# Last-layer layernorm variance from chunk sums in a bidirectional minGRU kernel: Squares on ScalarE and accumulating DMAs for four turned token tiles

## The chip, the cores and the metric

One core of a Trainium2 chip runs the whole kernel. The time is the device time of one execution in microseconds (us). TensorE is called PE in the profile (its weight loads PEld), VectorE DVE, ScalarE ACT, GpSimd POOL and SyncE SP. All data are float32. "A measurement" of the kernel before is a median of 3 executions: 1724.67 us, from 1724.2 to 1725.33.

## What is computed

Eight items of 512 tokens with 512 features (B = 8, S = H = 512) go through a block of two residual branches. The part that the change touches is the first branch, a stack of four bidirectional minGRU layers, fused by one matrix. Cut to what matters:

```python
def _mingru(x, Wz, bz, Wh, bh):
    z = sigmoid(einsum('bsi,hi->bsh', x, Wz) + bz)
    h_tilde = tanh(einsum('bsi,hi->bsh', x, Wh) + bh)
    a = clip(1.0 - z, CLAMP_LO, CLAMP_HI)
    return _linear_scan(a, z * h_tilde)          # h_t = a_t * h_(t-1) + z_t * h~_t

def _stack(x, ...):
    h = x
    for i in range(4):
        h_new = _mingru(h, Wz[i], bz[i], Wh[i], bh[i])
        if i > 0:
            h_new = h_new + h
        h = _layernorm(h_new, gamma, beta)
    return h

h_comb = concatenate([_stack(x), flip(_stack(flip(x)))], axis=-1)
x = x + einsum('bsi,hi->bsh', h_comb, fusion_W) + fusion_b      # x is normalised ahead of the stack
x = x + ffn(_layernorm(x))                                      # ternary weights, GELU, layernorm
```

The same matrix serves as Wz and Wh here, and both directions share their weights. The layernorm after the last layer needs, for each token, the mean and the variance over 512 features. The kernel folds the mean into the fusion weights, so that only 1/sqrt(variance + 1e-5) of each token is left to find; fusion multiplies its result with it.

## The kernel before

A stream is one item in one direction, `(b, d)`; there are 16. Its state `h` is kept transposed: features on the partitions, in four chunks of 128, and the 512 tokens along the free axis, since the scan runs over tokens. The layernorm between layers wants the features along the free axis. So each of the four tiles of 128 tokens is "turned" (four PE transposes into one PSUM bank `pt`, `turned`, L294), DVE takes its statistics (`stats`, L153: BN_STATS, aggregate, and the addition of eps; POOL raises to the power -0.5), ACT writes the normalised token tile, and four more transposes turn it "back" (ACT evicts the bank `pf` with gamma and beta, L316).

The order of the work is written out by hand as a series of steps: `slot` (L407) is one step, and `now[0]` counts them. The instructions are put on each engine's queue in exactly this order. In one step: the gate chunk of one stream (`gates`, L422: eight PE matmul instructions into `u`; ACT computes `a`, `t` and `z` from it, `factors`, L441), then what is due of the two queues `turns` and `backs` (`shares`, at most `cap` of each, as soon as their step has come), then on DVE the product `z*t` and the scan of the chunk (`product`, `scan`), then what was put off as "resid", then the closing work on ACT of the turns and backs (the eviction of `pf`, the normalised token tile). ACT may run ahead of DVE by as many chunks as there are buffers of `a` (3) and `t` (2); PE may run ahead of ACT by four buffers of `u`.

Items go in pairs. Within a pair the streams come in the order (b, 0), (b, 1), (b+1, 0), (b+1, 1), four gate chunks each, so a layer of a pair takes 16 steps. In the last layer (L520) the residual sum of a stream can't be added chunk by chunk, because `h` is still read by the gates of the later chunks; so the sums `h[c] += z[c]` come one a step from the step of the stream's last gate chunk on, in "resid". They are done in place, and `h` is the input of fusion. `norm_last` (L339) then queues four turns, from the fifth step after the last gate chunk on, one a step: transposes, statistics, and the power into column `t` of `rsv`. No token tile is written. In the same steps the turns of items to come (`norm_x`, statistics of `x` for the first layer, tile `x`) and, in the first pair, small pieces that prepare the ternary weights (`pieces`; ACT: absolute values of `pwa`) are mixed in.

`fusion` (L533) follows, four steps an item (16 PE matmul instructions each, `pu`), and in the pairs before the last the steps of the next pair's first layer are put between them. `need` (L273) at the start of an item's fusion makes steps of turns alone until no turn of its two streams is left. DVE then adds `pu * rsv` to the row of `x`, and SP stores it. After the last pair the FFN runs to the end of the kernel; it is not touched.

The buffers that the change touches: `tok` (10 tiles of 128 x 512, counted in `held`), `z` (16 tiles, counted in `zlive`), `ps_t` (2 PSUM banks). No DMA is issued by POOL.

Of the kernel before, what the change touches and what calls it, by code (L numbers as in the profile page):

```python
# [9 lines left out]
F32 = mybir.dt.float32  # L10
F32R = mybir.dt.float32r
AF = mybir.ActivationFunctionType
ALU = mybir.AluOpType
AX = mybir.AxisListType
PSUM = bass.MemoryType.PSUM

P = 128
LN_EPS = 1e-5
# [6 lines left out]
def kernel(  # L25
# [26 lines left out]
    nc = tc.nc  # L52
    B, S, H = x.shape
    L = gru_wT.shape[0]
    F = fc_wT.shape[1]
    NC_ = H // P
    NT = S // P
# [7 lines left out]
    small = ctx.enter_context(tc.tile_pool(name="small", bufs=8))  # L65
# [4 lines left out]
    tokp = ctx.enter_context(tc.tile_pool(name="tok", bufs=TOK))  # L70
# [48 lines left out]
    for i in range(2):  # L119
        s = const.tile([P, P], F32, name=f"fpick{i}")  # L120
# [24 lines left out]
    ident = const.tile([P, P], F32, name="ident")  # L145
# [3 lines left out]
    mhalf = const.tile([P, 1], F32, name="mhalf")  # L149
# [3 lines left out]
    def stats(src, name, rs=None, shift=True):  # L153

        st = small.tile([P, 6], F32, tag="st", name=f"st_{name}")
        nc.vector.bn_stats(st, src)  # L156
        mv = small.tile([P, 2], F32, tag="mv", name=f"mv_{name}")
        nc.vector.bn_aggr(mv, st)  # L158
        if rs is None:
            rs = small.tile([P, 1], F32, tag="rs", name=f"rs_{name}")  # L160
        ve = small.tile([P, 1], F32, tag="ve", name=f"ve_{name}")
        nc.vector.tensor_scalar(ve, mv[:, 1:2], LN_EPS, None, ALU.add)
        nc.gpsimd.tensor_tensor(rs, ve, mhalf, ALU.pow)  # L163
        if not shift:
            return rs, None
        nmu = small.tile([P, 1], F32, tag="nmu", name=f"nmu_{name}")
        nc.vector.tensor_scalar(nmu, mv[:, 0:1], -1.0, None, ALU.mult)  # L167
        return rs, nmu

    def normalise(dst, src, rs_nmu, name):  # L170
        rs, nmu = rs_nmu
        nmr = small.tile([P, 1], F32, tag="nmr", name=f"nmr_{name}")
        nc.scalar.activation(nmr, nmu, AF.Copy, scale=rs)
        nc.scalar.activation(dst, src, AF.Identity, bias=nmr, scale=rs)  # L174
# [39 lines left out]
    with rec:  # L214
        gp = rec.enter_context(tc.tile_pool(name="gate", bufs=3))
        ps_u = rec.enter_context(tc.tile_pool(name="ps_u", bufs=4, space=PSUM))
        ps_t = rec.enter_context(tc.tile_pool(name="ps_t", bufs=2, space=PSUM))
# [4 lines left out]
        now = [0]  # L222
        state = {}
        rsv = {}
        turns, backs = [], []

        held = [0]
# [32 lines left out]
        zlive = [0]  # L260

        left = {}

        def queue(q, key, at, piece, go):
            left[key] = left.get(key, 0) + 1
            q.append((at, piece, key, go))
# [6 lines left out]
        def need(*keys):  # L273

            while any(left.get(k) for k in keys):
                slot(None, 2)

        def tokens(source, tok, rs, name):

            def go():  # L280
                src = source()
                found = stats(src, name, rs, tok is not None)
                if tok is None:
                    return lambda: None
                held[0] += 1

                def last():
                    tile_ = tokp.tile([P, H], F32, tag="tok", name=f"tok_{name}")
                    normalise(tile_, src, found, name)
                    tok.append(tile_)  # L290
                return last
            return go

        def turned(zs, t, name, frees=0):  # L294
            def source():
                if t == NT - 1:
                    zlive[0] -= frees
                spare = name.startswith("00_0") and t > 1
                pt = (ps_f if spare else ps_t).tile([P, H], F32, tag="pf" if spare else "pt", name=f"pt_{name}")
                for c in range(NC_):  # L300
                    nc.tensor.transpose(pt[:, ts(c, P)], zs[c][:, ts(t, P)], ident)  # L301
                return pt
            return source
# [21 lines left out]
        def norm(s, zs, tag, pause, pair=1):  # L325

            toks, at = Tokens(), now[0] + pause

            def dst():
                if s not in state:  # L330
                    state[s] = hp.tile([P, NC_, S], F32, tag="h", name=f"h_{s[0]}{s[1]}")
                return state[s]

            for t in range(NT):
                queue(turns, s, at, t // pair, tokens(turned(zs, t, f"{tag}_{t}", NC_), toks, None, f"{tag}_{t}"))
            for c in range(NC_):
                queue(backs, s, toks, c // pair, back(toks, dst, c, True, f"{tag}_{c}"))

        def norm_last(s, tag):  # L339
            rsv[s] = small.tile([P, NT], F32, tag="rsv", name=f"rsv_{tag}")  # L340
            zs = [state[s][:, c, :] for c in range(NC_)]
            for t in range(NT):
                queue(turns, s, now[0] + NC_ + 1, t, tokens(turned(zs, t, f"{tag}_{t}"), None, rsv[s][:, t : t + 1], f"{tag}_{t}"))

        rx, scale = {}, {}

# [44 lines left out]
        stages = []  # L391
# [15 lines left out]
        def slot(work=None, cap=1, long=False):  # L407

            end = work() if work is not None else None
            due("factors")  # L410
            if long:
                due("scans")
            last = shares(cap) + x_shares()
            due("scans")
            if end is not None:
                end()
            due("resid")
            for f in last:
                f()
            now[0] += 1  # L420
# [82 lines left out]
        def layer(s, l):  # L503
            while s not in state:
                slot(None, 2)
            need(s)
            zs = []
            h = state[s]
            for o in range(NC_):
                def scans(a, z, o=o):  # L510
                    scan(z, a, z, s[1] == 1)
                    zs.append(z)
                    if l < L - 1:
                        nc.vector.tensor_tensor(z, z, h[:, o, :], ALU.add)  # L514
                    elif o == NC_ - 1:

                        for c in range(NC_):
                            def sums(c=c):
                                zlive[0] -= 1
                                nc.vector.tensor_tensor(h[:, c, :], zs[c], h[:, c, :], ALU.add)  # L520
                            stages.append((now[0] + c, "resid", sums))
                slot(gates(h, l, o, f"{s[0]}{s[1]}_{l}_{o}", scans))

                if s[0] < 2 and (l == L - 1 or o % 2) and len(extra) > 2 * NW or s == (B - 2, 1) and l == L - 1:
                    pieces(1)
            now[0] -= 1
            if l < L - 1:
                norm(s, zs, f"{s[0]}{s[1]}_{l}", 2)
            else:
                norm_last(s, f"{s[0]}{s[1]}_{l}")  # L530
            now[0] += 1

        def fusion(b):  # L533
            hs, rs = [], []

            def tile_of(t):
                def work():
                    if t == 0:
                        need((b, 0), (b, 1))
                        hs.extend(state.pop((b, d)) for d in range(2))  # L540
                        rs.extend(rsv.pop((b, d)) for d in range(2))
                    row = xs["f", b, t]
                    nc.vector.tensor_tensor(row, row, fb, ALU.add)
                    pieces((1, 2, 1, 0, 2, 2, 2, 2)[t + (b % 2) * NT])
                    pus = []
                    for d in range(2):
                        pu = ps_u.tile([P, H], F32, tag="u", name=f"pu_{b}_{t}_{d}")
                        for c in range(NC_):
                            nc.tensor.matmul(  # L549
                                pu, lhsT=hs[d][:, c, ts(t, P)], rhs=fw[:, d * NC_ + c, :],  # L550
                                start=(c == 0), stop=(c == NC_ - 1),
                            )
                        pus.append(pu)

                    def end():
                        for d in range(2):
                            nc.vector.scalar_tensor_tensor(
                                row, pus[d], rs[d][:, t : t + 1], row, ALU.mult, ALU.add
                            )
                        nc.sync.dma_start(out=x1[b][t], in_=row)  # L560
                    return end
                return work
            return [tile_of(t) for t in range(NT)]


        sums = {n: const.tile([P, NW], F32, name=f"sums_{n}") for n in ("fc", "pw")}
# [187 lines left out]
    for i in range(2):  # L754
        s = const.tile([P, P], F32, name=f"pick{i}")
# [132 lines left out]
    for j in range(ends):  # L888
        b, k = divmod(j, NF)
# [81 lines left out]
```

## Time and profile before

| | |
|---|---|
| median of 3 executions | 1724.67 us |
| the profiled execution | 1725.0 us, of which 1723.0 us from the first to the last instruction |
| granted PE clock | 1.000 |
| GRU part, fusion included | up to about 1228 us |
| FFN part | from about 1228 us to the end |

The last layer from its first residual sum to the start of fusion, one stretch for each pair:

| pair, stretch (us) | PE busy | DVE busy | ACT busy | POOL busy |
|---|---|---|---|---|
| first, 224 to 277 | 53.00 | 47.73 | 35.06 | 8.09 |
| second, 524 to 576 | 51.72 | 46.87 | 26.29 | 8.01 |
| third, 823 to 875 | 52.00 | 46.88 | 26.96 | 7.99 |
| fourth, 1121 to 1173 | 51.39 | 49.21 | 31.14 | 6.52 |

Busy time counts overlapping instructions once. [...]

How to read the lines: a group row of the page gives line, engine, operation, output <- input, shapes and count, then busy time, the mean of one in ns, the idle time just before it and what ended that. A timeline row gives start, duration, engine, line, operation, and in brackets the idle time before it with its releaser. A row of the chain gives start, duration, engine and line of one piece of the chain of work that ended last.

### The profile page before, as it was taken

How to read it: one execution, taken by the hardware profiler on the slowest of the kernel's cores; microseconds unless marked ns; L12 is line 12 of the kernel's file. 1: busy time of each engine (PE TensorE's matmuls, PEld its weight loads, DVE VectorE, ACT ScalarE, POOL GpSimd, SP SyncE). 2: the span in 40 equal slices, each digit the busy share in tenths (PEclk: the TensorE clock that was granted, in tenths of full speed). 3: DMA queues.
4: the chain of work that ended last, by engine and by line, in shares of the span. 5: the costliest groups of instructions: out<-in, count | busy, mean ns of one | idle time of the engine just before them, and what ended most of it. 6: DMA issues, size and time to landing. Idle time of an engine off the chain costs nothing.

```text
span 1723.0 us, 19728 instructions
## 1 busy us (share of the span) xinstructions
PE 1704.6 (99%) x6424; PEld 1039.2 (60%) x6424; DVE 1452.1 (84%) x2865; ACT 1067.0 (62%) x1836; POOL 214.6 (12%) x334
## 2 busy tenths in 40 slices
PE   8999999999999999999999999999999999999998
PEld 4455554455555445555544555554688888888887
DVE  7989989889998998999899899996468778768876
ACT  3898883468886245888624688861266566566654
POOL 2111111111111111111111111111000000000000
PEclk9999999999999999999999999999999999999999
DMA  7002221250000125000012201102201101101100
GB/s 269 19 25 80 98 86 43 68 189 1 1 13 19 55 68 189 1 1 17 14 55 80 92 10 40 74 1 97 75 1 50 49 1 49 50 12 39 49 19 31
DMA packets 46454, 91.73 MB, mean 53 GB/s; under 512 B 5264, under 2 KB 5264, under 8 KB 45328
## 3 DMA queue, kind: packets, MB, share of 16 engines
q1 hardware_dynamic: 45488, 88.91, 15.3%
q10 hardware_dynamic: 864, 1.57, 0.3%
q8 instruction: 50, 0.82, 0.2%
q14 instruction: 52, 0.43, 0.1%
HBM read 65.30 MB, written 25.17 MB: 53 GB/s over the span
## 4 chain that ended last, share of the span: by engine, by line
PE 75%; DVE 19%; issue 4%; ACT 1%; POOL 0%; DMA 0%; DVEq 0%; POOLq 0%
PE u L427 29%; PE ph L788 12%; PE po L815 12%; PE pu L549 9%; PE pt L301 5%; DVE z L455 4%; PE pf L310 4%; PE u L470 3%; DVE st L156 3%; DVE z L451 2%; DVE zf L455 1%; DVE a L450 1%; DVE mv L158 1%; PE py L199 1%; DVE z L514 1%
## 5 line engine op out<-in xcount | busy, mean ns | idle before, releaser
L427 PE MATMUL u<-h,gw 128*128 128x512 f32 x768 | 345.5, 592 | 0.0
L427 PE MATMUL u<-xT,gw 128*128 128x512 f32 x768 | 345.4, 592 | 0.0
L455 DVE TENSOR_TENSOR_SCAN z<-a,z 128x512 f32<-128x512 f32 x224 | 274.1, 1224 | 7.6
L792 ACT ACTIVATE g<-ph 128x512 f32<-128x512 f32 x128 | 76.4, 597 | 242.1 <-PE ph L788 242.1
L427 PEld LDWEIGHTS u<-h,gw 128*128 128x128 f32 x768 | 138.7, 190 | 139.2 <-issue 138.7
L427 PEld LDWEIGHTS u<-xT,gw 128*128 128x128 f32 x768 | 138.7, 190 | 139.2 <-issue 138.0
L444 ACT ACTIVATE a<-u,ngb 128x512 f32<-128x512 f32 x192 | 131.5, 685 | 143.0 <-PE u L427 142.5
L163 POOL TENSOR_TENSOR rs<-ve,mhalf 128x1 f32<-128x1 f32 x192 | 123.0, 641 | 713.4 <-DVE nmu L167 656.9
L156 DVE BATCH_NORM_STATS2 st<-pt 128x6 f32<-128x512 f32 x256 | 177.1, 692 | 40.3 <-PE pt L301 39.8
L815 PE MATMUL po<-pwq,ghi 128*128 128x512 f32 x512 | 203.5, 397 | 0.0
L788 PE MATMUL ph<-yhi,fcq 128*128 128x512 f32 x512 | 199.7, 390 | 0.0
L815 PE MATMUL po<-pwq,glo 128*128 128x512 f32 x512 | 199.6, 390 | 0.0
L788 PE MATMUL ph<-ylo,fcq 128*128 128x512 f32 x512 | 199.4, 389 | 0.0
L451 DVE TENSOR_TENSOR z<-z,t 128x512 f32<-128x512 f32 x224 | 153.4, 685 | 8.5 <-ACT z L446 8.3
L174 ACT ACTIVATE tok<-pt,nmr,rs 128x512 f32<-128x512 f32 x192 | 149.2, 777 | 6.4
L803 DVE TENSOR_TENSOR acc<-acc,g 128x512 f32<-128x512 f32 x112 | 77.3, 690 | 87.9 <-ACT g L792 86.9
L446 ACT ACTIVATE z<-u,gb 128x512 f32<-128x512 f32 x192 | 132.2, 689 | 0.0
L445 ACT ACTIVATE t<-u,gb 128x512 f32<-128x512 f32 x192 | 130.7, 681 | 0.0
L301 PEld LDWEIGHTS pt<-ident,z 128*128 128x128 f32 x640 | 78.4, 141 | 82.4 <-issue 47.5
L549 PE MATMUL pu<-fw,xT 128*128 128x512 f32 x256 | 115.2, 593 | 0.0
L549 PE MATMUL pu<-fw,h 128*128 128x512 f32 x256 | 115.1, 592 | 0.0
L470 PE MATMUL u<-xT,gw 128*128 128x512 f32 x256 | 114.6, 593 | 0.3 <-DVE gw L672 0.3
(138 smaller groups left out, 2550.7 us busy)
## 6 DMA issues: line engine op xcount, KB each, us to landing
xn<-in_x_dram SPq DMA_DIRECT2D x32, 256.0 KB, 4.6
xf<-in_x_dram SPq DMA_DIRECT2D x32, 256.0 KB, 6.2
x<-xf SPq DMA_DIRECT2D x32, 256.0 KB, 2.0
xy<-x SPq DMA_DIRECT2D x32, 256.0 KB, 4.3
out_dram<-xy SPq DMA_DIRECT2D x32, 256.0 KB, 2.0
xT<-in_xt_dram SPq DMA_DIRECT2D x7, 1024.0 KB, 7.7
fca<-in_fc_wT_dram SPq DMA_DIRECT2D x16, 256.0 KB, 2.9
pwa<-in_proj_wT_dram SPq DMA_DIRECT2D x16, 256.0 KB, 2.6
```

Of the source, the lines that this page charges most:

```text
L156: nc.vector.bn_stats(st, src)
L174: nc.scalar.activation(dst, src, AF.Identity, bias=nmr, scale=rs)
L301: nc.tensor.transpose(pt[:, ts(c, P)], zs[c][:, ts(t, P)], ident)
L427: nc.tensor.matmul(u, lhsT=gw[l][:, c, ts(o, P)], rhs=h[:, c, :], start=(c == 0), stop=(c == NC_ - 1),)
L444: nc.scalar.activation(a, u, AF.Sigmoid, bias=ngb[:, l, o : o + 1], scale=-1.0)
L446: nc.scalar.activation(z, u, AF.Sigmoid, bias=gb[:, l, o : o + 1])
L451: nc.vector.tensor_tensor(z, z, t, ALU.mult)
L455: nc.vector.tensor_tensor_scan(dst[:, d], a[:, d], z[:, d], 0.0, ALU.mult, ALU.add)
L470: nc.tensor.matmul(u, lhsT=gw[0][:, c, ts(o, P)], rhs=xT[b][:, c, :], start=(c == 0), stop=(c == NC_ - 1),)
L549: nc.tensor.matmul(pu, lhsT=hs[d][:, c, ts(t, P)], rhs=fw[:, d * NC_ + c, :], start=(c == 0), stop=(c == NC_ - 1),)
L788: nc.tensor.matmul(ph, lhsT=w, rhs=ys[b][c][i], start=(c == 0 and i == 0), stop=(c == NC_ - 1 and i == 1),)
L815: nc.tensor.matmul(po[b][t], lhsT=part[:, ts(t, P)], rhs=pwq[k // NP_][:, k % NP_, :], start=(k == 0 and i == 0), stop=(k == NF - 1 and i ...
```

## The change

In the last layer the variance is found from sums over the chunks. As soon as a chunk's residual sum is there, ACT squares it into the chunk's `z` tile, which is free by then. The four chunks are added elementwise into a tile `total_`, and the four squares into the first `z` tile: DVE adds the first two chunks, and accumulating DMAs, issued by POOL, add the rest (two for `total_`, three for the squares), one step after the chunk's sum. What is left to sum over are the 128 partitions: two turns a stream (one of `total_`, one of the squares) instead of four, each followed by one reduction over the turned features on DVE, which gives all four token tiles at once. The mean of squares less the squared mean is the variance. `need` is no longer called by fusion, which instead asserts that the turns are through before their result is read.

```diff
-        def norm_last(s, tag):
-            rsv[s] = small.tile([P, NT], F32, tag="rsv", name=f"rsv_{tag}")
-            zs = [state[s][:, c, :] for c in range(NC_)]
-            for t in range(NT):
-                queue(turns, s, now[0] + NC_ + 1, t, tokens(turned(zs, t, f"{tag}_{t}"), None, rsv[s][:, t : t + 1], f"{tag}_{t}"))
+        def square_sums(s, zs, h, tag):
+            total_, sq = [], zs[0]
+
+            def chunk(c):
+                def go():
+                    nc.vector.tensor_tensor(h[:, c, :], zs[c], h[:, c, :], ALU.add)
+                    nc.scalar.activation(zs[c], h[:, c, :], AF.Square)
+                    if c == 1:
+                        total_.append(tokp.tile([P, S], F32, tag="tok", name=f"sum_{tag}"))
+                        held[0] += 1
+                        nc.vector.tensor_tensor(total_[0], h[:, 0, :], h[:, 1, :], ALU.add)
+                    if c:
+                        stages.append((now[0] + 1, "resid", add(c)))
+                return go
+
+            def add(c):
+                def go():
+                    if c > 1:
+                        nc.gpsimd.dma_start(out=total_[0], in_=h[:, c, :], accum_op=ALU.add)
+                    nc.gpsimd.dma_start(out=sq, in_=zs[c], accum_op=ALU.add)
+                    zlive[0] -= 1
+                return go
+
+            for c in range(NC_):
+                stages.append((now[0] + c, "resid", chunk(c)))
+            rs = rsv[s] = small.tile([P, NT], F32, tag="rsv", name=f"rsv_{tag}")
+            su = small.tile([P, 2, NT], F32, tag="su", name=f"su_{tag}")
+
+            def turn(i):
+                def go():
+                    pt = ps_t.tile([P, H], F32, tag="pt", name=f"ps_{tag}_{i}")
+                    src = sq if i else total_[0]
+                    for t in range(NT):
+                        nc.tensor.transpose(pt[:, ts(t, P)], src[:, ts(t, P)], ident)
+                    nc.vector.tensor_reduce(su[:, i, :], pt.rearrange("p (t f) -> p t f", t=NT), AX.X, ALU.add)
+                    if i == 0:
+                        held[0] -= 1
+                        return lambda: None
+                    zlive[0] -= 1
+                    nc.vector.tensor_scalar(su, su, 1.0 / H, None, ALU.mult)
+                    var = small.tile([P, NT], F32, tag="var", name=f"var_{tag}")
+                    nc.vector.tensor_tensor(var, su[:, 0, :], su[:, 0, :], ALU.mult)
+                    nc.vector.tensor_tensor(var, su[:, 1, :], var, ALU.subtract)
+                    nc.vector.tensor_scalar(var, var, 0.0, LN_EPS, ALU.max, ALU.add)
+                    nc.gpsimd.tensor_tensor(rs, var, mhalf.broadcast_to([P, NT]), ALU.pow)
+                    return lambda: None
+                return go
+
+            for i in range(2):
+                queue(turns, s, now[0] + NC_ + 1, i, turn(i))
...
                     elif o == NC_ - 1:
-                        for c in range(NC_):
-                            def sums(c=c):
-                                zlive[0] -= 1
-                                nc.vector.tensor_tensor(h[:, c, :], zs[c], h[:, c, :], ALU.add)
-                            stages.append((now[0] + c, "resid", sums))
+                        square_sums(s, zs, h, f"{s[0]}{s[1]}_{l}")
...
-            now[0] -= 1
             if l < L - 1:
+                now[0] -= 1
                 norm(s, zs, f"{s[0]}{s[1]}_{l}", 2)
-            else:
-                norm_last(s, f"{s[0]}{s[1]}_{l}")
-            now[0] += 1
+                now[0] += 1
...
                     if t == 0:
-                        need((b, 0), (b, 1))
                         hs.extend(state.pop((b, d)) for d in range(2))
...
                     def end():
+                        assert not any(left[b, d] for d in range(2))
                         for d in range(2):
```

The turns come in the same step as before (the fifth after the last gate chunk): `square_sums` is called inside that chunk's step, where `now[0]` is already what `norm_last` was given.

## The prediction

> **What bounds the kernel now.** I read the page first (busy shares, chain), then the chain of waits and the timelines of the last layer, and last the group rows for prices.
>
> ```profile
> PE 1704.6 (99%) x6424; PEld 1039.2 (60%) x6424; DVE 1452.1 (84%) x2865; ACT 1067.0 (62%) x1836; POOL 214.6 (12%) x334
> PE 75%; DVE 19%; issue 4%; ACT 1%; POOL 0%; DMA 0%; DVEq 0%; POOLq 0%
> ```
>
> PE is the bound and DVE is close behind it. The chain of waits in the first pair's last layer shows what a step of PE is there: eight gate matmuls and one group of four transposes, with no gap.
>
> ```profile
> 244.56 0.44 PE pt L301 x4
> 245.00 3.43 PE u L427 x8
> 248.43 0.44 PE pt L301 x4
> 248.87 3.44 PE u L427 x8
> ```
>
> So a step costs PE 3.87 us, and a transpose group 0.44. The timeline of the second pair's last layer shows ACT and DVE beside it:
>
> ```profile
> 531.38 0.67 DVE L520 TENSOR_TENSOR xT<-z,xT 128x512 f32<-128x512 f32 x1
> 532.04 0.69 ACT L444 ACTIVATE a<-u,ngb 128x512 f32<-128x512 f32 x1 [1.42 <-PE u L427]
> 532.63 0.68 ACT L445 ACTIVATE t<-u,gb 128x512 f32<-128x512 f32 x1
> 533.20 0.69 ACT L446 ACTIVATE z<-u,gb 128x512 f32<-128x512 f32 x1
> 533.77 0.79 ACT L316 ACTIVATE h<-pf,bet,gam 128x512 f32<-128x512 f32 x1
> 533.92 0.69 DVE L451 TENSOR_TENSOR z<-z,t 128x512 f32<-128x512 f32 x1 [0.73 <-ACT z L446]
> 534.64 1.23 DVE L455 TENSOR_TENSOR_SCAN z<-a,z 128x512 f32<-128x512 f32 x1
> 535.79 0.67 DVE L520 TENSOR_TENSOR xT<-z,xT 128x512 f32<-128x512 f32 x1
> 535.91 0.69 ACT L444 ACTIVATE a<-u,ngb 128x512 f32<-128x512 f32 x1 [1.36 <-PE u L427]
> ```
>
> ACT takes a chunk as soon as PE has it (a, t, z), and then waits for nothing but PE: it starts the next a at 535.91 while DVE still works on L520 (535.79 to 536.46). DVE's product, scan and residual sum come after ACT's z, in that order. That ACT may run ahead of DVE is what lets a step last 3.87 us. The residual sums give a clock: in step 0 (the last gate chunk of the pair's first stream) and step 12 (that of its fourth) L520 starts at 224.56 and 275.69, 524.06 and 574.85, 823.42 and 874.21, 1121.67 and 1171.57. Twelve steps take 51.1, 50.8, 50.8 and 49.9 us.
>
> Prices:
>
> ```profile
> L794 ACT ACTIVATE sq<-g 128x512 f32<-128x512 f32 x128 | 81.1, 633 | 4.1
> L827 DVE TENSOR_REDUCE su<-pst 128x4 f32<-128x512 f32 x16 | 10.2, 682 | 0.0
> L156 DVE BATCH_NORM_STATS2 st<-pt 128x6 f32<-128x512 f32 x256 | 177.1, 692 | 40.3 <-PE pt L301 39.8
> x<-xf SPq DMA_DIRECT2D x32, 256.0 KB, 2.0
> xf<-in_x_dram SPq DMA_DIRECT2D x32, 256.0 KB, 6.2
> ```
>
> [...] ACT's nmr stands waiting for POOL's rs 50 times (73.7 us), with gates queued behind it. [...] the built program has two table loads before and after. [...] the trace's Square has 633, which I use. [...]
>
> **The change, part by part.**
>
> *Turns.* Each of 16 streams loses four transpose groups and gets two: 32 x 0.44 = 14.0 us off PE. On DVE four turns of 1.08 us (556.22 from 555.14: stats, aggregate, eps) go, 4.3 us; two reduces (1.3 for both in the trace at 1294), four small operations (0.8) and one sum of two chunks (0.6) come, 2.7. DVE gains 1.6 a stream, 25 in all. POOL loses 64 pows of 0.63 and gets 16 of about 1.0 (L834).
>
> *Steps of turns alone.* They exist once, ahead of the last item's fusion: two steps with four groups (1197.29 to 1200.46), PE waiting 0.63 and 0.35 us for DVE. They go; two groups stand in the fusion step instead. In the other pairs the turns were already through, so nothing goes.
>
> *Squares.* This decides. In the order of the built program the Square of step k stands on ACT after a, t, z of step k and before a, t, z of step k+1, and it waits for DVE's residual sum of step k. That sum is behind the scan of step k, which is behind ACT's z of step k. So from step 0 ACT can no longer run ahead: z, product, scan, sum, Square, next a. One turn of the loop, from sum start to sum start: sum 0.67, hand-over 0.04, Square 0.54 (1401.77 to 1402.31, the next instruction overlapping), a to product 1.88 (532.04 to 533.92), product and scan 1.87 (533.92 to 535.79): 5.0 us against PE's 3.87. Queued behind the waiting Square are the next gates (PE soon has its four u buffers full), the back evictions and the normalised tokens.
>
> Other work in ACT's queue between a Square and the next a lengthens the loop: in pairs 1 and 2 (counting from 0) six evictions of 0.66, two nmr and tok of 1.0, two scale copies of 0.5, 7.0 in twelve steps, and 0.5 in step 6, where DVE has sum, reduce, four small operations and x statistics ahead of the product. Pair 0 has no such 0.5, but twelve weight pieces (pwa, 0.52 to 0.71 with the accumulator read; 0.66): 7.0 + 7.9. Pair 3: six evictions, three tokens, four yhi of 0.5: 9.0. Twelve steps then take
>
> - pair 0: 60.0 + 14.9 = 74.9, before 51.1: +23.8
> - pairs 1 and 2: 60.0 + 7.5 = 67.5, before 50.8: +16.7 each
> - pair 3: 60.0 + 9.0 = 69.0, before 49.9: +19.1
>
> *Accumulating DMAs.* Five a stream on POOL, each waiting for the one before on the same tile and for DVE's sum or ACT's Square. Behind them on POOL stand only the rx pows (wanted steps later) and the stream's own last pow. PE waits for the landing at its first transposes, two steps after the last sum. Landing costs between 2.0 us (x<-xf, plain) and 6.2 (xf, the slowest such row), or some 12 if adding doubles that; it can only add a wait, not save one. I take 3.5 with the issue[...]. Step 5's group then runs 3.6 us after step 3's sum; gate chunk 6 is ready 3.9 later, and ACT wants it two loops and a Square (10.6 us) after that sum. The landing may take 6.7 us before it costs there. In step 13 both turns of the third stream stand together: PE gets past them about 0.5 us after step 12's sum. Before, PE was at step 14 at 276.25, 575.75, 875.27 and 1175.81, which is -0.1, +0.2, +0.4 and +3.6 us from that sum's end. This corrects the four numbers to 24.4, 17.0, 16.8 and 16.0: together 74.2.
>
> *Given back after step 14.* Pairs 0 to 2 have four groups fewer there (1.75) and lose some 0.5 of PE's short waits for tokens, as DVE is lighter: 2.3 each. Pair 3 has 6 groups and 0.98 of waits less, 2 groups more: 2.7. In all 9.6. The steps in which the next items' first layer is mixed in are limited by PE and DVE alike; their Squares wait for sums that are nearly done.
>
> Sum: 74.2 - 9.6 = 64.6 us. The profiled execution took 1725.0 (span 1723.0 and 2.0 around it), 0.3 above the median of 1724.67. Forecast: 1789 us.
>
> **Rivals.**
>
> - *PE stays the bound (faster).* If a Square found its sum ready, only PE's savings would count: 14.0 + 0.98 off, 1710. For it: PE is 99% busy, and ACT idles 1.4 us a step. Against it: the idle time ends with PE's chunk, and the sum can't start before z of the same step, 1.87 us later. It decides only if the loop is under PE's new 3.65 us a step (3.43 and half a group of 0.44); its parts would have to lose a quarter. 5%.
> - *The landing binds as well (slower still).* If an accumulating DMA takes 10 us from sum to transposes, PE is 3.3 late in two streams of a pair and 6.4 in the third, in part the same wait: some 10 a pair, 1830. For it: no such DMA in the trace, two queued a step on POOL. Against: 6.7 us of room. 17%.
> - *Only part arrives.* Where DVE was late anyway (its chain runs from 506 to 632 in pair 1), its 1.6 us a stream may return all, not 2.3 a pair, and pair 0's weight pieces may fall in the wait of a Square: 12 to 25 us less, 1765 to 1775, or 1745 if evictions hide too. 14%.
> - *The change does what it says:* the counts of the built program confirm two groups a stream and no steps of turns alone.
>
> **How the numbers follow.** The loop with its extras has 63%, within about 20 us of 1789. The lower end, 1755, takes in most of the partial case, the upper, 1825, half of the late landing. Slower by over 0.2% (3.4 us, about what a measurement can tell from none): 63 + 17 + 14 = 94%; faster 5%; within 0.2% 1%.
>
> **What would show it.** In the changed profile ACT's Square should stand waiting for DVE's sum with 1.9 to 2.6 us of idle time nearly each step, sums should follow each other every 5.0 us and more in the last layer, the chain should alternate between ACT and DVE there, and PE should idle some 60 us, mostly at the groups fed by DMA or at u. The FFN should be unchanged. It is wrong if the sums stay 3.9 to 4.3 us apart; if PE's waits for DMA landings are longer than the Square's part, the landing is the cause.

## The result, and the profile after

The kernel after takes 1799.55 us (1797.71 to 1800.94 in 4 runs), the kernel before 1724.43 us (1723.97 to 1725.33): ratio 1.043, 95% interval 1.042 to 1.0445. The forecast was 1789 us, range 1755 to 1825: slower, as forecast, and 10.6 us above the forecast number. The profiled execution has a span of 1795.9 us, 72.9 more than before.

The page of the kernel after (busy shares, then the chain that ended last) answers to the first two lines shown of before:

```profile
PE 1711.6 (95%) x6296; PEld 1034.9 (58%) x6296; DVE 1439.1 (80%) x2785; ACT 1101.8 (61%) x1900; POOL 260.1 (14%) x366
...
PE 66%; DVE 20%; ACT 6%; issue 5%; DMA 2%; POOL 0%; DVEq 0%; SPq 0%; POOLq 0%
```

PE had 99% before, and no engine is full any more. PE has 128 instructions fewer than before and yet is busy for 7 us longer; why is seen below. The view of the waits (who waited for whom: us in total, times, longest) has two rows for ACT that did not exist before:

```profile
ACT z L348 <- DVE h L347: 91.2, 29, 7.2
ACT z L348 <- DVE xT L347: 88.0, 32, 4.0
```

L348 is the Square and L347 the residual sum. 61 of 64 Squares wait, 179.2 us in all. The timeline of the second pair's last layer, ACT and DVE (start, duration, instruction, in brackets the idle time before it):

```profile
547.50 0.68 ACT L492 ACTIVATE a<-u,ngb 128x512 f32<-128x512 f32 x1
548.07 0.69 ACT L493 ACTIVATE t<-u,gb 128x512 f32<-128x512 f32 x1
...
548.64 0.70 ACT L494 ACTIVATE z<-u,gb 128x512 f32<-128x512 f32 x1
549.36 0.69 DVE L499 TENSOR_TENSOR z<-z,t 128x512 f32<-128x512 f32 x1 [0.73 <-ACT z L494]
550.09 1.22 DVE L503 TENSOR_TENSOR_SCAN z<-a,z 128x512 f32<-128x512 f32 x1
551.23 0.67 DVE L347 TENSOR_TENSOR xT<-z,xT 128x512 f32<-128x512 f32 x1
551.93 0.63 ACT L348 ACTIVATE z<-xT 128x512 f32<-128x512 f32 x1 [2.60 <-DVE xT L347]
```

ACT is done with z at 549.34 and stands for 2.60 us until the sum is there. The next a starts at 554.12, behind the Square, an eviction and a token tile. In the kernel before, the next a started while DVE was still at the sum. The chain of waits shows the same as a ring; this is a later step of that pair, in which nothing else stands in ACT's queue:

```profile
582.45 0.59 DVE h L347
...
583.07 0.63 ACT z L348
583.70 0.58 ACT a L492
584.27 0.58 ACT t L493
584.85 0.59 ACT z L494
...
585.46 0.70 DVE z L499
...
586.19 1.22 DVE z L503
587.41 0.58 DVE h L347
```

From one sum to the next it is 4.96 us. PE is not in the ring. What PE does meanwhile is seen in its waits:

```profile
PE pf L310 <- ACT tok L174: 26.5, 6, 7.7
PE ps L375 <- DMA sum<-h: 19.7, 3, 8.4
PE ps L375 <- DVE xT L347: 10.9, 1, 10.9
PE ps L375 <- DMA sum<-xT: 6.4, 5, 4.6
```

It stands for tokens that are queued on ACT behind a Square, and at the turns (L375), for the accumulating DMAs and what they add up. And in the table of stretches (length, then busy time of PE, PEld, DVE, ACT, POOL, with counts; then the granted PE clock, DMA share, GB/s) the last layers of the four pairs have a lower clock than the stretches between them and the FFN, which have 1.00:

```profile
223.59:299.00 75.41, 55.59 (x151) 26.40 (x150) 47.07 (x83) 43.37 (x86) 18.27 (x22) 0.86 0.49 108
544.00:615.00 71.00, 55.94 (x155) 27.07 (x154) 47.12 (x82) 35.89 (x61) 18.17 (x22) 0.88 0.34 60
860.00:930.00 70.00, 54.91 (x158) 26.96 (x157) 47.48 (x83) 36.12 (x61) 18.16 (x22) 0.90 0.34 60
1174.00:1245.00 71.00, 54.73 (x161) 26.43 (x159) 47.70 (x81) 37.34 (x64) 15.94 (x19) 0.93 0.34 64
```

The time was lost in the last layers. The FFN, from 1300 to the end, has 495.9 us against 495.0 before (from 1228).

### The profile page after: what moved, and what is told of

Same layout as the page of the kernel before. It is cut to its first block, busy times and chain, and to the rows that moved or that the text cites. A ratio compares the mean times of both kernels' runs of the same rounds, so it can differ in the third digit from the quotient of the medians.

```text
span 1795.9 us, 19570 instructions
## 1 busy us (share of the span) xinstructions
PE 1711.6 (95%) x6296; PEld 1034.9 (58%) x6296; DVE 1439.1 (80%) x2785; ACT 1101.8 (61%) x1900; POOL 260.1 (14%) x366
## 4 chain that ended last, share of the span: by engine, by line
PE 66%; DVE 20%; ACT 6%; issue 5%; DMA 2%; POOL 0%; DVEq 0%; SPq 0%; POOLq 0%
PE u L475 22%; PE ph L830 11%; PE po L857 11%; PE pu L589 9%; DVE z L503 5%; PE u L518 4%; PE pf L310 3%; DVE z L499 3%; PE pt L301 3%; DVE st L156 2%; DVE zf L503 1%; DVE a L498 1%; ACT a L492 1%; ACT z L348 1%; ACT z L494 1%
## 5 line engine op out<-in xcount | busy, mean ns | idle before, releaser
L475 PE MATMUL u<-h,gw 128*128 128x512 f32 x768 | 357.9, 611 | 0.0
L475 PE MATMUL u<-xT,gw 128*128 128x512 f32 x768 | 344.7, 593 | 0.0
L475 PEld LDWEIGHTS u<-h,gw 128*128 128x128 f32 x768 | 145.0, 198 | 151.2 <-issue 150.7
L834 ACT ACTIVATE g<-ph 128x512 f32<-128x512 f32 x128 | 76.5, 597 | 216.6 <-PE ph L830 216.6
L156 DVE BATCH_NORM_STATS2 st<-pt 128x6 f32<-128x512 f32 x192 | 132.9, 692 | 33.3 <-PE pt L301 32.6
L310 PE MATMUL pf<-ident,tok 128*128 128x128 f32 x768 | 113.8, 274 | 28.6 <-ACT tok L174 26.5
L498 DVE TENSOR_SCALAR a<-a 128x512 f32<-128x512 f32 x224 | 93.8, 419 | 52.3 <-ACT a L492 52.2
```

Source lines behind the costliest of these rows:

```text
L310: nc.tensor.transpose(pf[:, ts(t, P)], toks[t][:, ts(c, P)], ident)
L475: nc.tensor.matmul(u, lhsT=gw[l][:, c, ts(o, P)], rhs=h[:, c, :], start=(c == 0), stop=(c == NC_ - 1),)
```

## The experiments

Two theories stood at the start: ACT's Square waits in its queue (the prediction's loop), or the accumulating DMAs hold PE (its landing rival). Each was measured beside runs of the kernel before on the same chip, with a median of 1725.1 us (e1 to e4, e9, e10) or 1725.2 us (e5 to e8).

**e1, no Squares.**

```diff
-                    nc.scalar.activation(zs[c], h[:, c, :], AF.Square)
```

> The changed kernel without the 64 Squares on ACT; all else stays, the accumulating DMAs too, which now add up the scan results instead of their squares (the variance is so left out, the work on the other engines is not). Theory 'Square waits in ACT's queue': the last layer goes back to PE's pace, sums 3.7 to 4.0 us apart, time 1710 to 1725 us (1724.4 less 15 of PE, plus up to 1 us for each of 16 landings that PE may now have to wait for). Theory 'landing of the DMAs and POOL's queue': little changes, 1780 us or more, and PE still waits some 20 to 30 us for DMAs.

Measured: 1748.0 us, ratio 1.013 (1.012 to 1.015). The ring is gone, but the time lies between what the two theories said.

**e2, no DMAs.**

```diff
-                    if c > 1:
-                        nc.gpsimd.dma_start(out=total_[0], in_=h[:, c, :], accum_op=ALU.add)
-                    nc.gpsimd.dma_start(out=sq, in_=zs[c], accum_op=ALU.add)
```

> The changed kernel without the 80 accumulating DMAs; Squares stay where they are. The sums over chunks 1 to 3 are left out, so two turns sum over part of the features. Theory 'Square waits in ACT's queue': the loop stays, sums 5.0 us and more apart, and only PE's waits at groups fed by DMA go: 1785 to 1797 us against 1799.5. Theory 'landing and POOL's queue': 1710 to 1730 us.

Measured: 1784.6 us, ratio 1.035 (1.033 to 1.037). Sums 4.96 us apart at the shortest, as in the kernel after.

**e3, neither** (both edits).

> Neither Squares nor accumulating DMAs: what is left of the change are the two turns instead of four and the end of the steps of turns alone (sums and squares over chunks are left out). Both theories: PE is the bound and loses 14.0 us of transposes and 1.0 us of waits, 1708 to 1711 us. If it isn't near that, DVE or ACT limits the last layer as well, and the price of 0.44 us a group is not all that counts.

Measured: 1709.2 us, ratio 0.991 (0.989 to 0.992), 15.9 us less than before.

The three and the kernel after make a square:

| | no DMAs | DMAs |
|---|---|---|
| no Squares | 1709.2 | 1748.0 |
| Squares | 1784.6 | 1799.6 |

The Squares cost 75.4 us by themselves, the DMAs 38.8; the DMAs add 15.0 where the Squares are there already. So both theories hold, the first for most of it. In e1, where PE is the bound, PE's waits at turns fed by DMA are these:

```profile
PE ps L374 <- DMA sum<-h: 16.0, 4, 5.4
PE ps L374 <- DMA sum<-xT: 7.8, 4, 4.9
...
PE ps L374 <- DMA z<-z: 1.2, 1, 1.2
```

That is 25.0 us. The rest is slower matmuls, at a mean granted clock of 0.991 for 0.999: e1 and e3 have the same 6296 PE instructions, and PE is busy with them for 1704.2 us in e1, 1689.5 in e3, 14.7 more. The spans differ by 39.6 us (1747.1 and 1707.5), which is 25.0 + 14.7 but for rounding.

**e4, each Square one step later on ACT, and the turns with it.**

```diff
-                    nc.scalar.activation(zs[c], h[:, c, :], AF.Square)
+                    stages.append((now[0] + 1, "resid", square(c)))
...
-                queue(turns, s, now[0] + NC_ + 1, i, turn(i))
+                queue(turns, s, now[0] + NC_ + 1 + lag, i, turn(i))
```

Here `square` does the Square and puts the DMA off to the step after; `lag` is 1, and 0 for the last stream of all, which keeps its Squares in place.

> The whole change with its full result, but each Square is put on ACT one step after its residual sum (behind a, t and z of the next step), its DMA one step after that, and the two turns one step later; the very last stream keeps the old steps. Theory 'Square waits in ACT's queue': the sum is done when ACT comes to the Square, so ACT runs ahead again and PE is the bound: 1708 to 1720 us. Rival 'ACT has 40 us more of work in the last layers' (64 Squares of 0.63 us), wherever it stands: 1745 to 1790. Theory 'landing and POOL's queue': no better than the change itself, 1790 or more.

Measured: 1739.8 us, ratio 1.008 (1.007 to 1.010). 59.7 us go without any work being taken away. How they divide between the Squares and the turns was not tried in this place; the later turns alone bring 14.6 us in the ring (e10 below). That the ring is gone is seen in its pace: the twelve steps of a pair's last layer take 52.0 to 55.1 us, where the kernel after takes 67.9 to 73.9 and e10 67.1 to 73.8. But e4 misses the 1708 to 1720: DMAs still hold PE for 21.3 us, as they did in e1. Two lines of the second pair, from POOL's timeline, show a wait that lies in the order of a queue:

```profile
545.99 0.67 POOL L163 TENSOR_TENSOR rx<-ve_x,mhalf 128x1 f32<-128x1 f32 x1 [5.93 <-DVE ve_x L162]
546.63 0.86 POOL L369 DMA_DIRECT2D sum<-xT  x1
```

The chunk that this DMA adds had its sum at 540.96 (its L348, the residual sum of e4, ran from 540.29 for 0.67). The DMA is due a step later, and in that step the power for the next pair's statistics of x comes first on POOL. PE stood from 548.12 to 549.96 for it.

**e5, as e4, but each DMA is issued in the step of what it adds.**

```diff
+                    if c > 1:
+                        nc.gpsimd.dma_start(out=total_[0], in_=h[:, c, :], accum_op=ALU.add)
...
-                        stages.append((now[0] + 1, "resid", add(c)))
+                        nc.gpsimd.dma_start(out=sq, in_=zs[c], accum_op=ALU.add)
```

> As e4_late_squares, but each accumulating DMA is issued in the step of what it adds (for the total: with the chunk's residual sum; for the squares: with the Square), not a step later. In e4 the total's last DMA of a pair's first and second stream stood on POOL behind an rx power that waited for the next step's statistics (546.63 us, though its sum was there at 540.96). Theory 'order on POOL': the DMA starts some 4 to 5 us sooner, PE's waits for DMAs shrink from 21 us to under 5 and the half-clock stretches after them go: 1709 to 1716 us. Rival 'the landing itself, 3.4 to 4 us, is too long for the two steps given': PE still waits 10 us or more, 1722 to 1738.

Measured: 1721.8 us, ratio 0.998 (0.997 to 0.999). PE's waits for DMAs fall from 21.3 to 7.5 us, 6.0 of them now for DMAs of the squares. Better by 18.0 us, and not all that was expected.

**e6, as e4, with the turns one more step later.**

```diff
-                queue(turns, s, now[0] + NC_ + 1 + lag, i, turn(i))
+                queue(turns, s, now[0] + NC_ + 1 + 2 * lag, i, turn(i))
```

> As e4_late_squares with its DMAs where e4 has them, but the two turns one more step later (two steps later than in the change; the very last stream keeps its steps). Any theory in which the wait is only that PE comes too early: 3.9 us more for each landing cover 1.4 to 3.9 of each wait of e4 (2.1, 5.1, 1.8, 4.5, 1.9, 4.5, 1.4 us): 2.4 us of waits stay, 1710 to 1717 us. If DMAs follow the turns (the power of one stream stands on POOL ahead of the next stream's DMAs), later turns delay them too and less is won: 1722 or more.

Measured: 1730.2 us, ratio 1.003 (1.002 to 1.004). PE's waits for DMAs are still 11.8 us. So PE's coming too early is not all. The other reading, by which DMAs and turns depend on each other through POOL, fits the number, but no run tried that dependence alone.

**e7, both.**

> Both: DMAs as in e5, turns as in e6. If PE is then never kept by a DMA: 1708 to 1711 us, the time of e3 without Squares and DMAs (1709.2). If ACT's 40 us of Squares cost something of themselves: 1713 or more.

Measured: 1715.0 us, ratio 0.994 (0.993 to 0.996): faster than both kernels. PE waits for no DMA at the turns, and the granted clock is 1.00. ACT runs ahead again; its timeline in the second pair's last layer (L363 is the Square):

```profile
531.57 0.69 ACT L498 ACTIVATE z<-u,gb 128x512 f32<-128x512 f32 x1
532.13 0.64 ACT L363 ACTIVATE z<-xT 128x512 f32<-128x512 f32 x1
532.66 0.78 ACT L316 ACTIVATE h<-pf,bet,gam 128x512 f32<-128x512 f32 x1
534.28 0.69 ACT L496 ACTIVATE a<-u,ngb 128x512 f32<-128x512 f32 x1 [0.84 <-PE u L479]
```

The Square starts with no wait, and ACT is the one that waits for PE, 0.84 us in this step. So the ring, and not the 40 us of work, made the kernel slow. The 64 Squares and 80 DMAs together still cost something: 5.8 us lie between this and e3, which has neither. 2.4 of it are longer waits of PE for token tiles (6.1 us against 3.7); the rest was not followed up.

**e8, the kernel before with the Squares and nothing else.**

```diff
                                 nc.vector.tensor_tensor(h[:, c, :], zs[c], h[:, c, :], ALU.add)
+                                nc.scalar.activation(zs[c], h[:, c, :], AF.Square)
```

> The kernel before with nothing added but the 64 Squares, at the change's place (behind each residual sum of the last layer, into the chunk's z tile); four turns a stream, no DMAs on POOL, the Squares' result unused. Theory 'Square waits in ACT's queue': the loop alone makes it slow, sums 5.0 us and more apart; e2 had 1784.6 us with two turns, and the two turns more cost only what stands outside the loop (9.6 us by the prediction): 1790 to 1797 us. If all 14 us of the transposes counted, 1799. If the Squares need the rest of the change to cost anything: 1725 to 1735.

Measured: 1794.2 us, ratio 1.040 (1.039 to 1.042). One instruction a chunk, whose result nobody reads, costs 69.0 us. And what e8 has more than e2, four turns for two, costs 9.6 us, not 14.

**e9, the kernel after with its DMAs issued at once** (L360 and L361 moved into `chunk`, behind the Square).

> The changed kernel with its Squares where they are, but each accumulating DMA issued in the step of what it adds instead of one step later (as in e5). What the DMAs cost beside the Squares is 15.0 us (1799.6 against 1784.6 in e2). Theory 'the DMAs are late because of their place in POOL's queue': most of it goes, 1785 to 1792 us. Theory 'the landing of 3.3 to 4 us itself': 1794 to 1800.

Measured: 1798.2 us, ratio 1.042 (1.041 to 1.044). So the place in POOL's queue is not what most of the 15 us are; the number lies where the landing itself was to put it. PE still waits 35.0 us at turns for DMAs of the totals (37.0 in the kernel after, the DVE row included). In the ring PE is so far ahead that it stands at the turn before the last sum has even been made. The second pair:

```profile
589.47 0.67 DVE L347 TENSOR_TENSOR h<-z,h 128x512 f32<-128x512 f32 x1
...
593.90 1.09 PE L370 MATMUL ps<-ident,sum 128*128 128x128 f32 x4 [7.07 <-DMA sum<-h]
```

PE stood from 586.83 to 593.90, and the sum ended at 590.14. An earlier issue can only shorten the second half of that.

**e10, the kernel after with its turns one step later.**

```diff
-                queue(turns, s, now[0] + NC_ + 1, i, turn(i))
+                queue(turns, s, now[0] + NC_ + (1 if s == (B - 1, 1) else 2), i, turn(i))
```

> The changed kernel with its Squares and DMAs where they are, but the two turns of each stream one step later (the very last stream keeps its step). PE has time to spare in the loop, so a turn a step later costs nothing there, and PE comes to it when the DMA has landed. If PE's standing still at the turn (and its half clock for some 5 us after it) is what the DMAs' 15 us consist of: 1786 to 1793 us. If the DMAs cost through POOL's queue or through the transfers as such: 1796 to 1800.

Measured: 1785.0 us, ratio 1.035 (1.033 to 1.036). That is the time of e2, which has no DMAs at all: with the turns one step later, the DMAs cost nothing that shows. PE still stands 22.1 us at the turns in e10, and these are free. So the 15 us lie at turns that PE reached before their DMA had landed. Why one landing was late where it cost most, which e10 changed as well, is taken up with the prediction below.

## Why the prediction was right, and where it was short

The clock of the prediction (starts of the residual sum in step 0 and step 12 of a pair's last layer) cuts every span into the same parts:

| us | before | after | e2, no DMAs | e10, later turns | e8, before with Squares |
|---|---|---|---|---|---|
| up to the first step 0 | 224.56 | 223.59 | 224.26 | 225.39 | 225.13 |
| twelve steps, pair 0 | 51.13 | 73.91 | 73.82 | 73.80 | 73.81 |
| pair 1 | 50.79 | 69.30 | 67.55 | 67.09 | 66.50 |
| pair 2 | 50.79 | 67.93 | 67.80 | 67.80 | 67.62 |
| pair 3 | 49.90 | 70.29 | 69.61 | 69.97 | 70.93 |
| three stretches between | 744.40 | 739.48 | 737.23 | 738.29 | 744.32 |
| from the last step 12 to the end | 551.43 | 551.40 | 541.73 | 541.96 | 544.33 |
| span | 1723.0 | 1795.9 | 1782.0 | 1784.3 | 1792.6 |

*Squares: right.* The loop was put at 5.0 us and is 4.96. With the extras in ACT's queue the twelve steps were forecast at +23.8, +16.7, +16.7 and +19.1, and came out at +22.8, +18.5, +17.1 and +20.4. The view that carried it was the order of the instructions on ACT together with one timeline of before: it showed how long after z the sum comes. PE's idle time was forecast at some 60 us more and is 65.9 more (84.3 against 18.4); it had named the tokens as queued behind the Squares, but not that PE would stand 26.5 us for them. That Square brings no table load is seen in the trace: ACT has two table loads of 1.28 us in the kernel after (L220 and L834), as many as in the kernel before (L220 and L792), and none at L348.

*Turns and steps of turns alone: right.* 14.0 + 0.98 us off PE were forecast where PE is the bound; e3 gained 15.9. That only 9.6 of it would come back beside the loop was forecast too, 6.9 in the first three pairs and 2.7 in the last. e8 against e2 gave 9.6, and in the table 7.1 in the stretches between and 2.6 in the last row.

*The sum for Squares and turns together* was 64.6 us. e2 has 59.5 (1784.6 - 1725.1). The forecast had too little coming back behind step 12: in the table e2 has 7.2 us less than before in the three stretches between and 9.7 less in the last one, 16.9 in all, where 2.1 (the correction of the step-14 starts) and 9.6 had been reckoned. e8, which still makes four turns, shows the term that was too small: the last pair. Its last row is 7.1 us below before, where the correction had 3.1. Why so much comes back there was not followed up.

*Accumulating DMAs: the usual landing right, the cost of zero wrong.* The landing was taken as 3.5 us with the issue, its author's estimate between the 2.0 and 6.2 us of other DMAs in the kernel before; the median is 3.3 for the total and 4.0 for the squares, of which two are queued together. Measured was a cost of 15.0 us. That is more than the 10.6 us by which the forecast fell short; by luck, the 5.1 us that the sum above had too many hid part of it.

The room of 6.7 us at the first two streams' turns nearly held: PE stood 10.9 us at a turn of pair 0, and the twelve steps took only 0.1 us more than in e2; in pair 1 they took 1.8 us more, in the others 0.1 and 0.7. What failed is the next sentence, "PE gets past them about 0.5 us after step 12's sum", and it failed in the last pair. PE was at step 14 at 299.23, 615.33, 929.85 and 1249.21, which is 1.06, 0.76, 0.77 and 4.04 us behind step 12's sum. In the last pair nothing follows that could hide it, and the table has 9.7 us between after and e2 in that one row. PE's timeline there:

```profile
1246.82 1.09 PE L375 MATMUL ps<-ident,sum 128*128 128x128 f32 x4 [4.58 <-DMA sum<-xT]
1248.33 1.09 PE L375 MATMUL ps<-ident,z 128*128 128x128 f32 x4 [0.42 <-DMA z<-z]
1249.21 5.50 PE L589 MATMUL pu<-fw,xT 128*128 128x512 f32 x8
1254.54 3.60 PE L589 MATMUL pu<-fw,h 128*128 128x512 f32 x8
```

PE stands 5.0 us for the two DMAs; then a group of four takes 1.09 us where 0.60 is usual, twice, and eight fusion matmuls 5.50 for 3.60, with a granted clock of 0.50 from 1246.19 to 1253.01. The DMA for which PE stands was itself late, as the timelines of SP and POOL show:

```profile
1235.40 0.33 SPq L651 DMA_DIRECT2D fcq<-wq_fc  x1
1235.78 0.86 POOL L360 DMA_DIRECT2D sum<-xT  x1 [1.28 <-PE u L475]
...
1243.34 0.86 POOL L360 DMA_DIRECT2D sum<-xT  x1 [4.99 <-DVE z L499]
```

L651 loads 1 MB of weights for the FFN. The total's DMA that was issued 0.38 us later landed after 7.0 us instead of 3.3, at 1242.81. Only then could the last one go to the same tile: it was issued at 1243.34, though its sum had been ready at 1240.21. The view names a product of DVE as what released it, but the issue comes 0.53 us behind that landing in e9 and e10 too, where no such product ends just before. With 3.3 us for both, the last one would have landed at about 1243.8, before step 12's sum was done at 1245.17 (an estimate: 1240.21, then 0.29 from a sum to its issue, as in the other pairs, and 3.34). In e9 the two met in the same way (the load at 1236.01, the DMA at 1236.38), and the DMA took 7.3 us: an earlier issue gained nothing there. In e10 the load came 3.8 us ahead of the DMA (1231.89 and 1235.69), and the DMA took 3.3 us. So e10 differs from the kernel after in two things in that pair, and how the 9.7 us divide between the meeting of the two transfers and the place of the turn was not tried. The prediction's 3.5 us had no other transfer beside it.

*Rivals.* "PE stays the bound" fell: it needs Squares that find their sums ready, which e7 has and the change has not. "The landing binds as well" was right in its mechanism in pair 3, where one landing took 7.0 us, and too dear as a whole (1830; it priced a landing of 10 us everywhere). "Only part arrives" fell: twelve steps brought all that was forecast, and the turns gave back their 9.6 us and no more. The mark set beforehand, that the landing is the cause if PE's waits for DMAs exceed the Square's part, would have misled in a closer case: idle time on PE is not a cost where ACT and DVE set the pace. In the kernel after 37.0 us of waits at the turns cost 15.0, and in e10 22.1 us cost nothing that shows.

## What to carry to other kernels

An instruction that goes to a queue with work for the next step, and waits for the last result of this step, ties two engines into a ring (here 4.96 us a step, where PE needed 3.87 in the kernel before); write down the ring's parts and add them up before asking whether the engine has time for the instruction. Putting it one step later takes the ring away at little cost (here, with the turns moved along, 1799.6 us became 1739.8, and 1715.0 once the transfers and turns behind it had their step too). When a result goes through a DMA, place its consumer in its queue by when the DMA lands, not by when the consumer's result is wanted: the engine stands where the instruction stands (PE for 7.07 us at one turn of e9). And look for what else is moving then: the landing beside a load of 1 MB took twice its usual time (7.0 us for 3.3).

## What the runs showed of the hardware

In the kernel after PE's granted clock was 0.50 for a time around the end of each of its stands of 4.58 us and more. In the second pair it stood 5.89 us for a token tile, and this is its timeline:

```profile
554.28 0.47 PE L310 MATMUL pf<-ident,tok 128*128 128x128 f32 x1 [5.89 <-ACT tok L174]
...
555.40 5.94 PE L475 MATMUL u<-h,gw 128*128 128x512 f32 x8
...
561.62 3.60 PE L475 MATMUL u<-h,gw 128*128 128x512 f32 x8
```

The first eight gate matmuls take 5.94 us, the next eight 3.60; the granted clock is 0.50 from 553.3 to 560.1 and 1.00 after that, so it came back 5.8 us behind the end of the stand. In consequence ACT waited 1.05 us for u at 561.38. From 224 us on there are eight such stretches at 0.50, of 6.8 to 13.7 us, and in each of them ends a stand of 4.58 to 10.91 us; the clock came back 3.6 to 6.2 us behind that end. Between them it was 1.00; the kernel before has a mean of 1.000. In the timelines of PE around the last layers of e2, e4, e9 and e10, too, every stand of 3.3 us or more was followed by slower matmuls, the shortest (3.30 us, e2, 616.74) by eight in 5.35 us. Two shorter ones differ: after a stand of 2.89 us (the kernel after, 1223.97) eight matmuls took 3.60 us at a clock of 1.00, but after one of 2.57 us in e5 they took 5.29:

```profile
245.80 3.60 PE L479 MATMUL u<-xT,gw 128*128 128x512 f32 x8
251.97 0.66 PE L379 MATMUL ps<-ident,z 128*128 128x128 f32 x4 [2.57 <-DMA z<-z]
252.47 5.29 PE L479 MATMUL u<-xT,gw 128*128 128x512 f32 x8
```

So the length of a stand alone does not tell here what it costs. Over the whole kernel after, the slow matmuls come to 20.9 us of PE time: 1711.6 us busy against 1690.7 in e7 with the same number of instructions. How much of it lies on the path was not tried by itself.

An accumulating DMA of 256 KB from SBUF to SBUF, issued by POOL, landed 3.2 us after its issue at the shortest in the kernel after, with medians of 3.3 (totals) and 4.0 us (squares). Beside the 1 MB load of the last pair two of them took 7.0 and 6.6 us (issued at 1235.78 and 1237.49); the longest elsewhere took 5.8 (629.58). The issue held POOL for 0.86 us, and for up to 1.22 where two followed each other.
